# Layer 0's GpSimd order pinned, layer 3's last queries projected beside attention's first stages: a four-layer kernel on one core

## The chip, the core and the metric

The kernel runs on one core of one Trainium2 chip. A core has a matrix engine (TensorE, PE in the profile; its weight loads are PEld), a vector engine (VectorE, DVE), an activation engine (ScalarE, ACT), GpSimd (POOL) and a queue engine (SyncE, SP) that issues DMA transfers. POOL issues transfers too, the indirect ones, which gather rows by an index. Each engine works through its own list of instructions in order, and waits at an instruction until the semaphores that it names have been raised by other engines or by transfers. So an instruction that waits holds everything behind it on its engine.

The metric is the device time of one execution in microseconds (us). Before the change three executions took 2797.17, 2802.5 and 2808.08 us, a median of 2802.5 us. The profiled execution took 2786.42 us. Its span, from the first to the last instruction, is 2784.6 us.

## The reference

x has 32 sequences of 64 tokens with 512 values, 2048 rows. Four layers are each added to x. Two matter here.

```python
# layer 0: cond, then an attention with rope and a mixture of experts
w = weights[subjects]                       # one 64x64 matrix per sequence
out = jnp.einsum('bct,bcd->bdt', x, w)
...
rms = jax.lax.rsqrt(jnp.mean(x * x, axis=-1, keepdims=True) + EPS)
h = x + attention(rmsnorm(x, ln1_w), ...)
out = h + moe(rmsnorm(h, ln2_w), ...)       # 1 shared expert, 2 of 7 routed ones

# layer 3: attention over a paged cache, window 256, then a product in int8
q, k = _rms(q, q_norm_scale), _rms(k, k_norm_scale)
q, k = _rope(q, pos), _rope(k, pos)
k_blocks = k_blocks.at[blk, :, off, :].set(k.transpose(0, 2, 1, 3))
v_blocks = v_blocks.at[blk, :, off, :].set(v.transpose(0, 2, 1, 3))
k_all = k_blocks[block_tables]...
p = jax.nn.softmax(scores, axis=-1)
```

So in layer 0 every pair of sequences needs a weight matrix that is gathered by an index, and in layer 3 every sequence needs the old rows of its cache window, with the new rows put over them.

## The kernel before

The 2048 rows are 16 tiles of 128 rows, two sequences each. The four layers run one after another. A tile framework writes the program: it allocates buffers from pools, adds the waits, and orders the instructions of each engine by its own planning. An instruction given to `pin` (`keep_in_program_order`) isn't moved past others that are so given on its engine; all others may be.

**Layer 0's front** (`layer0`, class `Front`) takes 16 tiles through 13 stages. The list `turns` gives each stage a lag: in step t the stage `mix` works on tile t, `qk_turn` and `scores` on tile t-1, `values`, `out_turn`, `out` and `out_norm` on t-2, `gate_up` and `down` on t-3. So TensorE always has another tile's products to do while one tile's results go through DVE, ACT and POOL.
- `mix` (L422) multiplies the tile by its weights `wbd`. `cond_weights` (L331) makes these on POOL: an indirect DMA brings 128 x 64 values as `wsel` (L284), and two multiplications by a mask (L338) lay them into the two halves of a 128 x 128 block-diagonal tile. `wsel` and `wbd` have two buffers each, and neither is pinned, so the planner put them one or two tiles ahead of their use.
- `rms_scaled` (L311) squares and sums on ACT (L316), forms the mean square `ms` on DVE (L318), raises it to -1/2 on POOL as `rstd` (L308), and scales on DVE (L321). It makes `xn` in `mix` and `hn` in `out`. `norm_turn` then transposes `xn` on TensorE (L414).
- `qkv` adds the two halves of the rope on POOL (L477, `qk`); `qk_turn` transposes the result on TensorE (L414, too).
- `out` adds x and h on POOL (L574).

After the front, experts are computed; layers 1 and 2 follow until 2282 us. In layer 1, `Bridge.work` uses `cond_weights` for its own weights.

**Layer 3** (`layer3`) has two parts. The first projects: `units` is a list of pairs (z, i), where z = 1 is the K/V projection of tile i and z = 0 its query projection; queries follow keys by `LAG` = 5 tiles. In turn u:
- the tile x is transposed (`turn`), and unit u is multiplied (L1803, four matmuls);
- `l3_length` (L1877) makes the norm of its heads: square on ACT, sum on DVE, power on POOL (L1887, `r`);
- unit u-2 is scaled and rotated (`l3_rotate`, L1891): `n` and `tc` on DVE, `ts` on POOL, and unit u-3 gets its sum `qkv` on DVE (L1912);
- a K/V unit's result is written to `newkv` in DRAM by SP (L1829), and for tiles 0 to 7 `old_rows` (L1739) gathers the three old chunks of one sequence's cache;
- a query's result is transposed to heads two turns later (`heads`).

The last five queries (tiles 11 to 15) are only multiplied and copied out as `qlate`; the generator `queries` normalizes, rotates and transposes them later, beside the attention, one of four pieces at every second step.

Then `new_rows` (L1751) gathers rows of `newkv` over the old ones, three gathers a sequence. Most of its indices lie out of bounds and bring nothing. Because it reads `newkv`, it waits for all 16 writes.

The second part is the attention (class `Attend`), in steps s of half a group: `keys` transposes a chunk of the cache (L1936) and makes the mask, `scores` multiplies (L1963) and takes scaled, masked scores and their minimum in one DVE instruction (L1970), then the exponential on ACT (L1974), the division on DVE (L1976, L1977); `turn0` and `turn1` transpose the probabilities (L1985), `values` multiplies by the values (L2010), `product` and its parts (L2032, L2047, L2054) do the output product and the int8 product. Score banks in PSUM are two.

Of the kernel before, what the change touches and what calls it, by code (L numbers as in the profile page):

```python
# [20 lines left out]
P = 128  # L21
# [159 lines left out]
class Prog:  # L181
# [120 lines left out]
            nc.vector.tensor_tensor(out, tp, scale.unsqueeze(2).to_broadcast([P, 4, P]), ALU.mult)  # L302
        return out

    def power(self, pool, src, which, name):

        out = pool.tile(list(src.shape), F32, name=name)
        self.nc.gpsimd.tensor_tensor(out, src, self.c(which)[:, : src.shape[1]], ALU.pow)  # L308
        return out

    def rms_scaled(self, pool, src, name):  # L311

        nc = self.nc
        junk = pool.tile([P, D], F32, name="junk")
        ss = pool.tile([P, 1], F32, name="ss")
        nc.scalar.activation(junk, src, AF.Square, accum_out=ss)  # L316
        ms = pool.tile([P, 1], F32, name="ms")
        nc.vector.tensor_scalar(ms, ss, 1.0 / D, 1e-5, ALU.mult, ALU.add)  # L318
        r = self.power(pool, ms, "nhalf", "rstd")
        out = pool.tile([P, D], F32, name=name)  # L320
        nc.vector.tensor_scalar(out, src, r, None, ALU.mult)  # L321
        return out
# [7 lines left out]

    def cond_weights(self, pool, src, idx, i, out=None):  # L331

        w = pool.tile([P, 64], F32, name="wsel")
        self.gather(w, self.a[src], idx[:, i : i + 1], later=out is not None)
        if out is None:
            out = pool.tile([P, P], F32, name="wbd")
        for k, half in enumerate(("lowhalf", "highhalf")):
            self.nc.gpsimd.tensor_scalar(out[:, 64 * k : 64 * k + 64], w, self.c(half), None, ALU.mult)  # L338
        return out


def layer0(g, w3, pool3):
# [51 lines left out]
class Front:  # L394
# [26 lines left out]

    def mix(self, i):  # L422
        g, nc, sb = self.g, self.g.nc, self.sb
        wbd = g.cond_weights(sb, "wc0", self.at, i)
        if i >= len(self.x):
            self.x.append(g.load_x(sb, g.a["x"], i, 5))
        x = self.x[i]
        o = self.ps.tile([P, D], F32, name="mix", tag="one")
        nc.tensor.matmul(o, wbd, x, start=True, stop=True)
        h = sb.tile([P, D], F32, name="h", bufs=4)  # L430
        nc.scalar.copy(h, o)
        self.keep(i, x=x, h=h, xn=g.rms_scaled(sb, h, "xn"))

    def norm_turn(self, i):
        (xn,) = self.take(i, "xn")
# [4 lines left out]
    def latents(self, i):  # L440
        nc, w = self.g.nc, self.w
        (xnT,) = self.take(i, "xnT")
        lp = self.ps.tile([P, 2, P], F32, name="lp", tag="one")
        for j in range(2):
            for c in range(4):
                nc.tensor.matmul(
                    lp[:, j, :], w["w_lat"][:, c, j * P : (j + 1) * P], xnT[:, c, :], start=c == 0, stop=c == 3
                )
        lat = self.sb.tile([P, 2, P], F32, name="lat")
        nc.scalar.copy(lat, lp)  # L450
        self.keep(i, lat=lat)

    def qkv(self, i):
        g, nc, sb, w = self.g, self.g.nc, self.sb, self.w
        xnT, lat = self.take(i, "xnT", "lat")

        qp = self.ps.tile([P, 2, D], F32, name="qp", tag="big", bufs=2)
        nc.tensor.matmul(qp[:, 0, :], lat[:, 1, :], w["w_q"], start=True, stop=True)
        kv = qp[:, 1, :].rearrange("p (h z d) -> p z h d", h=16, z=2)
        nc.tensor.matmul(  # L460
            kv[:, 0], lat[:, 0, :], w["w_kn"].rearrange("p (h d) -> p h d", h=16), start=True, stop=True
        )
        for c in range(4):
            nc.tensor.matmul(
                kv[:, 1], xnT[:, c, :], w["w_kr"][:, c, :].rearrange("p (h d) -> p h d", h=16),
                start=c == 0, stop=c == 3,
            )
        r = qp.rearrange("p z (h d) -> p (z h) d", h=16)
        qk = sb.tile([P, 32, 32], F32, name="qk")
        nc.scalar.copy(qk[:, :, 0:16], r[:, :, 0:16])  # L470
        cos = g.c("cos").unsqueeze(1).to_broadcast([P, 32, 16])
        sin = g.c("sin").unsqueeze(1).to_broadcast([P, 32, 16])
        nc.vector.tensor_tensor(qk[:, :, 16:32], r[:, :, 16:32], cos, ALU.mult)
        t2 = sb.tile([P, 32, 16], F32, name="t2")
        nc.vector.tensor_tensor(t2[:, :, 0:8], r[:, :, 24:32], sin[:, :, 0:8], ALU.mult)
        nc.vector.tensor_tensor(t2[:, :, 8:16], r[:, :, 16:24], sin[:, :, 8:16], ALU.mult)
        nc.gpsimd.tensor_tensor(qk[:, :, 16:32], qk[:, :, 16:32], t2, ALU.add)  # L477


        vp = self.ps.tile([P, 2, 256], F32, name="vp", tag="one")  # L480
        for b in range(2):
            for odd in range(2):
                nc.tensor.matmul(
                    vp[64 * odd : 64 * odd + 64, b, :], lat[:, 0, 64 * b : 64 * b + 64],
                    w["w_v"][:, 256 * odd : 256 * odd + 256], start=True, stop=True,
                )
        v = sb.tile([P, 2, 256], F32, name="v", bufs=3)
        nc.scalar.copy(v, vp)
        self.keep(i, qk=qk, v=v)
# [501 lines left out]
class Bridge:  # L991
# [11 lines left out]
    def work(self):  # L1003
        g = self.g
        for i in range(NT):
            g.cond_weights(self.pool, "wc1", g.at1, i, self.weights[i])
            yield
        for i in range(NT):
            self.x.append(self.g.load_x(self.pool, self.xs, i, NT, True))
            yield  # L1010
# [698 lines left out]


LAG = 5


def layer3(g, w, xs, xb):
# [3 lines left out]
    with ExitStack() as ctx:  # L1718
# [18 lines left out]
        kvs = []  # L1737

        def old_rows():  # L1739
            b = len(kvs)  # L1740
            if b == B:
                return
            kv = []
            for c in range(3):
                t = cache.tile([CH, D], F32, name="kvt")
                col = c * B + b
                g.gather(t, a["kv"], w["gidx"][0:CH, col : col + 1], later=True)
                kv.append(t)
            kvs.append(kv)

        def new_rows(b):  # L1751
            if b < B:
                for c in range(3):
                    col = c * B + b
                    g.gather(kvs[b][c], new, w["oidx"][0:CH, col : col + 1], bound=N - 1)

        with ExitStack() as c1:
            xp = c1.enter_context(tc.tile_pool(name="l3x", bufs=4, reuse_waits="tile"))
            for part in (slice(0, 4), slice(4, NT)):
# [2 lines left out]
            sb = c1.enter_context(tc.tile_pool(name="l3pj", bufs=2, reuse_waits="tile"))  # L1762
            ps = c1.enter_context(tc.tile_pool(name="l3pq", bufs=3, space=PSUM, reuse_waits="tile"))
            units = [
                (z, i) for t in range(NT + LAG) for z, i in ((1, t), (0, t - LAG)) if 0 <= i < NT
            ]
            xT, held, turned = {}, [], {}

            def turn(i):
                if i < NT:  # L1770
                    xT[i] = g.transpose4(ps, sb, x[i], "xT3", bufs=3, keep=LAG + 3, pin=True)
                    fetch(i + 4)

            def heads(ps, i, q):
                tp = ps.tile([P, 4, P], F32, name="tp", tag="tp", bufs=3)
# [10 lines left out]
            for u in range(len(units) + 5):  # L1786
# [10 lines left out]
                if u < len(units):  # L1797
# [18 lines left out]
                        held.append((pp, out, l3_length(g, sb, pp[:, 0:256])))  # L1816
                    else:
                        held.append((pp, out, l3_length(g, sb, pp)))
                if 0 <= u - 2 < len(units) and held[u - 2]:
                    z, i = units[u - 2]  # L1820
                    pp, out, r = held[u - 2]
                    held[u - 2] = l3_rotate(
                        g, sb, out[:, 0:256] if z else out, pp[:, 0:256] if z else pp, r, tab[z][:, i]
                    )
                if 0 <= u - 3 < len(units) and held[u - 3]:
                    z, i = units[u - 3]
                    out = held[u - 3]()
                    if z:
                        nc.sync.dma_start(out=new[i * P : (i + 1) * P, :], in_=outs[u - 3])  # L1829
                        if i < 8:  # L1830
                            old_rows()
                    else:
                        turned[u - 3] = out
                if u - 5 in turned:
                    heads(ps, units[u - 5][1], turned[u - 5])
            new_rows(0)
# [6 lines left out]
        def queries():  # L1843

            for i, q in slow:
                r = l3_length(g, s1, q)
                yield
                add = l3_rotate(g, s1, q, q, r, tab[0][:, i])
                yield
                add()  # L1850
                yield
                heads(ps, i, q)
                yield

        beside = queries()
        f = Attend(g, w, sb, ps, kvs, qT, xb)

        last = 2 * B - 1
        for s in range(-3, last + 8):
            if s % 2 == 0:  # L1860

                if s >= 4:
                    old_rows()
                new_rows(s // 2 + 4)
            elif s == -3:
                new_rows(2)
            for stage, at in (("keys", s + 3), ("turn0", s), ("scores", s + 2), ("turn1", s)):
                if 0 <= at <= last:
                    getattr(f, stage)(at)
            f.out()  # L1870
            if s >= 2 and s % 2 == 0:
                next(beside, None)
# [1 line left out]
                f.values(s - 1)  # L1874


def l3_length(g, sb, src):  # L1877

    nc = g.nc
    m = src.shape[1] // 64  # L1880
# [3 lines left out]
    nc.vector.tensor_reduce(ss, sq, AX.X, ALU.add)  # L1884
    nc.vector.tensor_scalar(ss, ss, 1.0 / 64, 1e-6, ALU.mult, ALU.add)
    r = sb.tile([P, m], F32, name="r3", bufs=3)
    nc.gpsimd.tensor_tensor(r, ss, g.c("nhalf")[:, 0:m], ALU.pow)  # L1887
    return r


# [204 lines left out]
```

## Time and profile before

The profile is a page about one execution, and a trace that can be asked for stretches of time. "Busy" is the time in which an engine worked, as seen by the profiler.

| what | us |
|---|---|
| median of three executions | 2802.5 |
| the profiled execution | 2786.42 |
| its span | 2784.6 |
| mean granted TensorE clock (1 is full) | 0.959 |

Some stretches, from the windows view, in us from the span's start:

| stretch | length | TensorE busy | DVE busy | ACT busy | POOL busy | granted clock |
|---|---|---|---|---|---|---|
| 0 to 30, layer 0's start | 30 | 7.38 | 2.83 | 2.96 | 8.59 | 1.00 |
| 70 to 280, layer 0's steady tiles | 210 | 199.66 | 128.43 | 85.47 | 49.36 | 1.00 |
| 280 to 370, its last full tiles | 90 | 87.77 | 57.52 | 36.83 | 16.75 | 1.00 |
| 2303 to 2335, layer 3's first units | 32 | 27.38 | 14.24 | 6.04 | 27.80 | 0.97 |
| 2335 to 2398, the later units | 63 | 63.00 | 45.00 | 15.26 | 49.20 | 0.96 |
| 2413 to 2438.4, between the parts | 25.4 | 9.19 | 4.84 | 8.28 | 19.59 | 0.61 |
| 2439 to 2785, the attention | 346 | 286.13 | 211.21 | 166.89 | 157.00 | 0.90 |

A line of a timeline gives the start in us, the busy time in us, the engine, the source line, the operation, what it writes and reads with the shapes, and how many instructions were merged; in brackets the idle time of the engine before it and what ended that idle time. DMA_INDIRECT on POOL is the issuing of a gather, not its transfer. A line of the waits view gives who waited for whom, the total, how many times, and the longest.

### The profile page before, as it was taken

What the parts mean: (1) busy time and instruction counts of PE and PEld (TensorE: products, weight loads), DVE (VectorE), ACT (ScalarE), POOL (GpSimd) and SP (SyncE); (2) the same over time, 40 slices, a digit from 0 to 9 for tenths busy, and PEclk for the clock granted to TensorE, in tenths of its full rate; (3) what the DMA queues carried; (4) which work ended last, traced back from release to release, by engine and by line L of the source; (5) the groups of instructions that cost most, each with busy time, mean ns of one, the idle gap of its engine ahead of it and who ended that gap; (6) DMA issues with size and microseconds to landing.
All of it is one profiled execution on the core that took longest, in us unless ns stands there. A gap on an engine that the chain in (4) does not pass through costs nothing.

```text
span 2784.6 us, 42002 instructions
## 1 busy us (share of the span) xinstructions
PE 2567.1 (92%) x16556; PEld 1640.1 (59%) x16571; DVE 1404.6 (50%) x3479; ACT 748.2 (27%) x1557; POOL 846.8 (30%) x904
## 2 busy tenths in 40 slices
PE   5999998997699999996899999999999999788878
PEld 4777765654555655654666666667666654344444
DVE  3666655734754333334455544445554416466656
ACT  2444430112211121111222222222222212354444
POOL 2222114624222223213122222222222108656550
PEclk9999999998699999998999999999999999889898
DMA  2233224446545965534010000001000025124340
GB/s 93 91 124 127 96 77 164 156 148 191 169 166 195 345 228 211 201 125 156 17 38 27 28 27 28 27 31 50 27 27 27 31 78 182 53 74 115 89 112 29
DMA packets 107078, 291.21 MB, mean 105 GB/s; under 512 B 20682, under 2 KB 21482, under 8 KB 99569
## 3 DMA queue, kind: packets, MB, share of 16 engines
q1 hardware_dynamic: 71232, 193.46, 19.5%
q0 software_dynamic: 35056, 89.13, 11.0%
q10 hardware_dynamic: 576, 5.77, 0.5%
q8 instruction: 135, 2.21, 0.3%
q14 instruction: 79, 0.64, 0.1%
HBM read 216.76 MB, written 87.56 MB: 109 GB/s over the span
## 4 chain that ended last, share of the span: by engine, by line
PE 48%; DVE 3%; issue 2%; POOL 1%; DMA 1%; another core or an unknown queue 1%; ACT 0%; SPq 0%; ACTq 0%; POOLq 0%; DVEq 0%
PE lp L1356 8%; PE out L1499 8%; PE zp L1433 8%; PE hp L1465 3%; PE gp L1488 2%; PE pp L1803 2%; PE y L2032 2%; PE op L2010 2%; PE sp L1963 2%; PE yp L1301 2%; PE pT L1985 2%; PE ep L1442 1%; PE kp L1936 1%; PE ap L1289 1%; PE csum L1452 1%
## 5 line engine op out<-in xcount | busy, mean ns | idle before, releaser
L910 PE MATMUL gu<-xT,wt 128*128 128x320 f32 x1472 | 407.1, 434 | 0.0
L910 PEld LDWEIGHTS gu<-xT,wt 128*128 128x128 f32 x1472 | 277.7, 191 | 119.5 <-issue 11.4
L1356 PEld LDWEIGHTS lp<-xnT,sb_mu 128*128 128x128 f32 x2048 | 235.7, 193 | 8.8 <-issue 6.7
L1356 PE MATMUL lp<-xnT,sb_mu 128*128 128x128 f32 x2048 | 238.6, 277 | 1.5 <-DVE xnT L256 0.8
L929 PE MATMUL y<-wt,hT 128*128 128x512 f32 (+1 forms) x552 | 238.7, 606 | 0.1
L1499 PE MATMUL out<-sb_w,gT 128*128 128x512 f32 x512 | 233.6, 599 | 0.0
L1433 PE MATMUL zp<-sb_w,xnT 128*128 128x512 f32 x512 | 226.5, 592 | 0.0
L1492 DVE COPY gT<-gp 128x512 f32<-128x512 f32 x64 | 44.3, 692 | 235.4 <-PE gp L1488 235.0
L284 POOL DMA_INDIRECT xr<-rows,stok x115 | 110.2, 958 | 154.7 <-PE tp L891 86.1
L1433 PEld LDWEIGHTS zp<-sb_w,xnT 128*128 128x128 f32 x512 | 93.7, 190 | 104.7 <-issue 100.9
L1499 PEld LDWEIGHTS out<-sb_w,gT 128*128 128x128 f32 x512 | 93.4, 190 | 103.5 <-issue 95.2
L929 PEld LDWEIGHTS y<-wt,hT 128*128 128x128 f32 (+1 forms) x552 | 80.0, 171 | 104.9 <-issue 88.4
L659 POOL TENSOR_TENSOR ga<-ga,sg 128x320 f32<-128x320 f32 x64 | 55.2, 863 | 283.4 <-ACT sg L655 281.3
L284 POOL DMA_INDIRECT yk<-ys,slot x96 | 99.5, 1036 | 123.9 <-SPq L798 65.2
L1510 POOL TENSOR_TENSOR xt<-xt,bc_bias 128x512 f32<-128x512 f32 x16 | 20.3, 1270 | 360.1 <-DMA x<-xt 360.1
L1470 ACT ACTIVATE h<-hp 128x512 f32<-128x512 f32 x128 | 69.5, 594 | 214.2 <-PE hp L1465 214.0
L1970 DVE CUSTOM_DVE_ANT_0 s<-sp,mask 128x336 f32<-128x336 f32 x128 | 61.4, 504 | 124.2 <-PE sp L1963 42.8
L284 POOL DMA_INDIRECT kvt<-kv,gidx x96 | 94.9, 989 | 93.6 <-PE op L2010 64.7
L1394 POOL TENSOR_TENSOR eT<-eT,inv 128x512 f32<-128x512 f32 x64 | 71.6, 1120 | 151.2 <-DVE inv L1393 149.3
L284 POOL DMA_INDIRECT kvt<-newkv,oidx x96 | 98.3, 1024 | 38.9 <-issue 29.9
L2032 PE MATMUL y<-sb_w_o,oT 128*128 128x512 f32 x128 | 74.4, 667 | 22.5 <-DVE y3s L1516 16.0
L891 PEld LDWEIGHTS tp<-sb_cst,xr 128*128 128x128 f32 x460 | 53.7, 147 | 65.4 <-issue 32.3
(379 smaller groups left out, 4616.2 us busy)
## 6 DMA issues: line engine op xcount, KB each, us to landing
wt<-w_e SPq DMA_DIRECT2D x32, 1538.0 KB
ys<-yo SPq DMA_DIRECT2D x115, 256.0 KB
ys<-zero SPq DMA_DIRECT2D x10, 2048.0 KB
xt<-x SPq DMA_DIRECT2D x62, 256.0 KB
wt<-w_e SPq DMA_DIRECT2D x7, 1536.0 KB
x<-xt SPq DMA_DIRECT2D x32, 256.0 KB
sb_w<-w SPq DMA_DIRECT2D x5, 1024.0 KB
rows<-hn SPq DMA_DIRECT2D x16, 256.0 KB
```

What stands on the lines that cost most here:

```text
L284: ins = self.nc.gpsimd.indirect_dma_start(out=out, out_offset=None, in_=src, in_offset=bass.IndirectOffsetOnAxis(ap=idx, axis=0), **kw)
L910: nc.tensor.matmul(o, wj[:, c, ic * P : (ic + 1) * P], xT[:, c, :], start=c == 0, stop=c == 3)
L929: nc.tensor.matmul(y[row : row + n, :], hTs[u][:, ic, col : col + n], wd[:, ic, :], start=ic == 0, stop=ic == 1,)
L1301: g.first(c, nc.tensor.matmul(yp, self.xT[:, c, :], w["w_2"][:, c, :], start=c == 0, stop=False))
L1356: g.first(e + c, nc.tensor.matmul(lp[:, e, :], w["mu"][:, c, (4 * q + e) * P : (4 * q + e + 1) * P], self.xnT[:, c, :], start=c == 0, stop ...
L1394: g.pin(nc.gpsimd.tensor_tensor(e3, e3, inv.unsqueeze(2).to_broadcast([P, 8, T]), ALU.mult))
L1433: g.first(c, nc.tensor.matmul(zp, self.xnT[:, c, :], w["w1"][:, c, cols], start=c == 0, stop=c == 3))
L1465: g.first(e + b, nc.tensor.matmul(hp[:, b, e, :], self.ews[q][r, e, :], self.z[q][r, e * P : (e + 1) * P], start=True, stop=True))
L1470: g.pin(nc.scalar.activation(self.hs[q][b], hp[:, b], AF.Gelu))
L1499: g.first(e, nc.tensor.matmul(self.out, self.gTs[q][:, e, :], w["w2"][:, 4 * q + e, :], start=q + e == 0, stop=q + e == 6 and q == 3))
L1970: nc.vector.tensor_tensor_reduce(p, sps[j], self.masks[2 * i + half], -0.0625, 3.0e38, ALU.add, ALU.min, m)
L2032: nc.tensor.matmul(yp, self.oT[i][:, c // 2, c % 2, :], w["w_o3"][:, c, :], start=c == 0, stop=c == 3)
```

## The change

In layer 0, `mix` no longer makes its own tile's weights. After it has given out the norm of tile i, it asks for the gather of tile i+1's weights (`weights`), and after `latents` of tile i the two multiplications lay them (`lay`). The gather, the multiplications, `rstd` of `xn` and the rope's sum `qk` on POOL are pinned. Tile 0's weights are made at once.

In layer 3:
- `old_rows` gathers one chunk instead of three, and is called once in every turn from 3 to 26, 24 times as before in sum; in the attention it is called three times where it was called once;
- `new_rows` is pinned;
- the queries of the last three tiles (`LAST`) are no longer units. Their x is transposed into parts of K's rope table that are no longer needed, and `project` multiplies them at the attention's steps -3, -2 and -1, with the banks of `y3` and `acc`;
- the last K/V unit is rotated one turn after its product instead of two, and in every turn the sums of older units are given out before the rotation of newer ones;
- `queries` takes five turns for a query instead of four, and its power on POOL is pinned.

```diff
     def mix(self, i):
         g, nc, sb = self.g, self.g.nc, self.sb
-        wbd = g.cond_weights(sb, "wc0", self.at, i)
+        if i == 0:
+            self.weights(0)
+            self.lay()
+        wbd = self.wbd
...
-        self.keep(i, x=x, h=h, xn=g.rms_scaled(sb, h, "xn"))
+        self.keep(i, x=x, h=h, xn=g.rms_scaled(sb, h, "xn", True))
+        self.weights(i + 1)
+
+    def weights(self, i):
+
+        self.asked = self.g.cond_weights(self.sb, "wc0", self.at, i) if i < NT else None
+
+    def lay(self):
+        if self.asked:
+            self.wbd = self.asked(self.sb.tile([P, P], F32, name="wbd"))
...
         self.keep(i, lat=lat)
+        self.lay()
...
-        nc.gpsimd.tensor_tensor(qk[:, :, 16:32], qk[:, :, 16:32], t2, ALU.add)
+        g.pin(nc.gpsimd.tensor_tensor(qk[:, :, 16:32], qk[:, :, 16:32], t2, ALU.add))
```

`cond_weights` and the power:

```diff
     def cond_weights(self, pool, src, idx, i, out=None):
 
         w = pool.tile([P, 64], F32, name="wsel")
-        self.gather(w, self.a[src], idx[:, i : i + 1], later=out is not None)
-        if out is None:
-            out = pool.tile([P, P], F32, name="wbd")
-        for k, half in enumerate(("lowhalf", "highhalf")):
-            self.nc.gpsimd.tensor_scalar(out[:, 64 * k : 64 * k + 64], w, self.c(half), None, ALU.mult)
-        return out
+        self.gather(w, self.a[src], idx[:, i : i + 1], later=True)
+
+        def lay(out):
+            for k, half in enumerate(("lowhalf", "highhalf")):
+                self.pin(self.nc.gpsimd.tensor_scalar(out[:, 64 * k : 64 * k + 64], w, self.c(half), None, ALU.mult))
+            return out
+
+        return lay
```

Layer 3:

```diff
         def old_rows():
-            b = len(kvs)
-            if b == B:
-                return
-            kv = []
-            for c in range(3):
-                t = cache.tile([CH, D], F32, name="kvt")
-                col = c * B + b
-                g.gather(t, a["kv"], w["gidx"][0:CH, col : col + 1], later=True)
-                kv.append(t)
-            kvs.append(kv)
+            if not kvs or len(kvs[-1]) == 3:
+                if len(kvs) == B:
+                    return
+                kvs.append([])
+            t = cache.tile([CH, D], F32, name="kvt")
+            col = len(kvs[-1]) * B + len(kvs) - 1
+            g.gather(t, a["kv"], w["gidx"][0:CH, col : col + 1], later=True)
+            kvs[-1].append(t)
...
-                    g.gather(kvs[b][c], new, w["oidx"][0:CH, col : col + 1], bound=N - 1)
+                    g.gather(kvs[b][c], new, w["oidx"][0:CH, col : col + 1], bound=N - 1, later=True)
...
-                (z, i) for t in range(NT + LAG) for z, i in ((1, t), (0, t - LAG)) if 0 <= i < NT
+                (z, i) for t in range(NT + LAG) for z, i in ((1, t), (0, t - LAG)) if 0 <= i < NT - (not z) * LAST
             ]
+            lag = [1 if unit == (1, NT - 1) else 2 for unit in units]
...
+                    j = 4 * (i - NT + LAST)
+                    xT[i] = tab[1][:, j : j + 4, :]
+                    g.evac(xT[i], tp)
...
+                for k, (z, i) in enumerate(units[: u + 1]):
+                    if not held[k]:
+                        continue
+                    if u == k + lag[k]:
+                        pp, out, r = held[k]
+                        held[k] = l3_rotate(
+                            g, sb, out[:, 0:256] if z else out, pp[:, 0:256] if z else pp, r, tab[z][:, i]
+                        )
+                    elif u == k + lag[k] + 1:
+                        out = held[k]()
+                        if z:
+                            nc.sync.dma_start(out=new[i * P : (i + 1) * P, :], in_=outs[k])
+                        else:
+                            turned[k] = out
+                if 3 <= u < 27:
+                    old_rows()
...
+        def project(i):
+
+            pp = ps.tile([P, D], F32, name="pp3", tag="y3" if i % 2 else "acc", bufs=1)
+            for c in range(4):
+                g.first(c, nc.tensor.matmul(pp, xT[i][:, c, :], wq[:, c, :], start=c == 0, stop=c == 3))
+            out = wp.tile([P, D], F32, name=f"qlate{i}")
+            nc.scalar.copy(out, pp)
+            slow.append((i, out))
...
+            if s == -3:
+                project(NT - LAST)
...
+            if -3 < s < LAST - 3:
+                project(NT - LAST + s + 3)
```

## The prediction

> **What bounds the kernel now.** I read the page's busy row first, then its slices, then the waits of TensorE, then the timelines of the two places where TensorE waits.
>
> ```profile
> PE 2567.1 (92%) x16556; PEld 1640.1 (59%) x16571; DVE 1404.6 (50%) x3479; ACT 748.2 (27%) x1557; POOL 846.8 (30%) x904
> PE   5999998997699999996899999999999999788878
> ```
>
> TensorE is the bound: 217 us of the span are left to it, and the second line, its busy tenths in 40 slices of 70 us, puts part of them at the very start and in the last seven slices. No matmul is removed, so only its waits can be won. The change touches layer 0's front (0 to 414 us) and layer 3 (2282 us to the end). TensorE's waits in the first 560 us, as (total, times, longest):
>
> ```profile
> PE tp L414 <- DVE xn L321: 22.9, 15, 8.5
> PE mix L429 <- DMA sb_w_v<-w_v: 12.8, 1, 12.8
> PE tp L414 <- POOL qk L477: 3.7, 1, 3.7
> ```
>
> The transpose of xn waits at nearly every tile. Why, POOL's timeline shows (start, us), at the first tiles and at a later one:
>
> ```profile
> 20.10 0.87 POOL L338 TENSOR_SCALAR wbd<-wsel,sb_cst 128x64 f32<-128x64 f32 x2 [3.02 <-DMA wsel<-wc,i_cond]
> 21.24 1.01 POOL L284 DMA_INDIRECT wsel<-wc,i_cond  x1 [0.27 <-POOL wbd L338]
> 22.28 0.60 POOL L308 TENSOR_TENSOR rstd<-ms,sb_cst 128x1 f32<-128x1 f32 x1
> 35.06 0.87 POOL L338 TENSOR_SCALAR wbd<-wsel,sb_cst 128x64 f32<-128x64 f32 x2 [12.18 <-PE mix L429]
> 36.21 1.04 POOL L284 DMA_INDIRECT wsel<-wc,i_cond  x1 [0.28 <-POOL wbd L338]
> 37.28 1.29 POOL L477 TENSOR_TENSOR qk<-qk,t 128x512 f32<-128x512 f32 x1
> 240.65 1.04 POOL L284 DMA_INDIRECT wsel<-wc,i_cond  x1 [0.28 <-POOL wbd L338]
> 241.71 0.60 POOL L308 TENSOR_TENSOR rstd<-ms,sb_cst 128x1 f32<-128x1 f32 x1
> ```
>
> rstd and qk, which TensorE waits for, stand behind weights of later tiles. In layer 3, TensorE, then POOL, then DVE:
>
> ```profile
> 2334.55 1.09 PE L1777 MATMUL tp<-sb_cst,qkv 128*128 128x128 f32 x4 [4.62 <-DVE qkv L1912]
> 2438.43 1.50 PE L1985 MATMUL pT<-sb_cst,s 128*112 128x128 f32 x6 [5.97 <-DVE s L1977]
> 2406.90 1.09 POOL L284 DMA_INDIRECT kvt<-newkv,oidx  x1 [0.39 <-issue]
> 2436.80 0.99 POOL L284 DMA_INDIRECT kvt<-newkv,oidx  x1 [0.30 <-issue]
> 2424.07 0.51 DVE L1970 CUSTOM_DVE_ANT_0 s<-sp,mask 128x336 f32<-128x336 f32 x1 [3.46 <-remote]
> 2430.40 0.51 DVE L1970 CUSTOM_DVE_ANT_0 s<-sp,mask 128x336 f32<-128x336 f32 x1 [5.81 <-remote]
> ```
>
> There is one stall of 4.62 us in the projections. Then, from 2413.0 to 2438.4, TensorE works 9.2 of 25.4 us. In it POOL issues 24 gathers of new rows without a break (2406.90 to 2437.8, one each 1.30 us), and DVE gets only six L1970 started (2418.43, 2419.84, 2424.07, 2430.40, 2433.90, 2437.46), though their scores lay ready; with the last gather it runs on. So what ends this gap is the end of the burst, and the burst's start is the landing of the last newkv write.
>
> **Layer 0, part by part.** The built order of the changed kernel on POOL is, for a tile: rstd of xn, gather of the next wsel, its two wbd halves, memset, x+h, rstd of hn, qk. No instruction is added.
> - First tile: ms is ready at 16.48 (DVE 16.33 + 0.15), rstd began at 22.28. It now follows wbd 0 at once: 5.8 us.
> - First qk: its operand t is ready at 34.89 (DVE 34.48 + 0.41), it began at 37.28, behind a wbd and a gather: 2.35 us of the 3.67 us wait. What is late next is mix 1, right ahead of it.
> - Tile 2: ms 54.89, rstd 55.99: 1.05 us of its 1.84.
> - The steady tiles: nine waits of 1.14 to 1.16 us (75.23 to 267.27). The last four tiles have no later weights to gather, so their rstd follows ms directly, and they wait 0.55 to 0.57. That is the changed order, already in this trace: 9 x 0.58 = 5.2 us. The rest, ACT's and DVE's chain from mix to xn, stays.
> - Against it: at tile 1 one scores matmul now precedes the xn transposes and waits for both copies (0.59 and 0.68 us, half seen): -0.8.
>
> Sum 13.6 us. The added wait is wbd's for its own wsel gather, just issued. Behind it on POOL stand memset, x+h and rstd of hn. The gather ends at 242.7 and x+h begins at 255.7: 13 us of cover. [...]
>
> **Layer 3's projections.** Old rows were three gathers in a run beside a K/V unit (for a pair of units POOL needs 3 x 1.25 + 1.04 + 0.72 + 1.63 + 1.26 = 8.4 us; TensorE 7.74). Now it is one a unit: 7.15 us a pair, and POOL keeps up. The 4.62 us wait goes: 4.6 us (bounds 2 to 4.6). [...] The row says: tc of 256 columns takes 0.42 us alone and 0.42 beside a gather (2306.20), but 1.14 beside POOL's own multiplication (2398.67). [...] I take 0. The last three transposed x go into rows of K's table that were read units ago: no wait.
>
> **The last K/V unit.** Its add ended on DVE near 2403.98, behind another unit's n, ss and tc (0.68, 0.67, 1.45 us); rotated a unit earlier it precedes them: 3.0 us (bounds 0 to 5). The write's landing (2.00) is unchanged, and SP's order is the same: from 2363 to 2404 it holds only such writes, so nothing stands before it. The pinned r of a late query now stands within the burst: -1.65 us, since the burst ends later by it. So the burst ends 4.6 + 3.0 - 1.65 = 6.0 us sooner.
>
> **The three late projections** (each 3.44 us of TensorE, 10.3 together) leave the front and go beside the burst. That by itself wins nothing: TensorE would only reach the wait sooner. It costs nothing either, for 16 us are idle there; without that cover the 10.3 us would merely return. But the first scores then come when gather 6 has landed, near 2410 (start 2399.3, five pitches of 1.30, 1.0 of issue, 3.0 of landing by the chain's row), not 2418, and DVE's trickle has 2 us more; its new order also does s0 and s1's divisions (1.8 us, done after the burst before). I take 2.5 us (bounds -2, as ACT's copies of qlate stand before its exponentials, to 7).
>
> For the clock, the row of granted clock from 2420 to 2460 us has 0.68, that is some 26 us at half. [...] The trace prices it less: from 2438.4 slow forms (kp 0.77 us for three) end at 2445.91 (0.51), 6 us of busy TensorE at half, so 3 us. [...]
>
> Layer 3: 6.0 + 2.5 = 8.5 us. The beside-work of the attention has five turns a query, done by step 50 instead of 40; the earliest need of the last is step 58. Its r of 1.65 us lie in POOL's idle 189 of 346 us: nothing.
>
> **Sum.** 13.6 + 8.5 = 22 us. Against the profiled execution (2786.4 us, span 2784.6) that gives 2764. The median of the runs is 2802.5, 16 us above that execution; taken from it, **2780**.
>
> **Rivals.**
> 1. *The burst decides alone* (0.18): the last write or the trickle doesn't come earlier, or the copies take back what they win. For: DVE starts one L1970 in 3.5 us whatever waits. Against: the write's place in the order is plain. Layer 0 alone, with 1 us: 2788.
> 2. *The gap closes further* (0.15): projections keep the clock up and softmax is well under way at the burst's end; layer 3 gives 16: 2772.
> 3. *POOL is blocked in layer 0* (0.05): wbd waits for a late wsel under the 2 MB zero writes, with hn's rstd behind it. It decides from a landing 14.6 us after issue (13 of cover, and 22 us of gain over 14 tiles); at 16 us: 2802.5 - 22 + 14 x 3 = 2822. Against: the longest such wait in the trace is 5.9 us.
> 4. *The order takes no effect* (0.03): 2800. Against: the built order shows it.
>
> The forecast has 0.59; its own range is 2770 to 2790. About 0.5% (14 us) is what runs of this kernel, 2797 to 2808, can tell from no change. From the cases: faster 0.82, same 0.13, slower 0.05. The range, 2762 to 2796, adds to the forecast's the second rival and most of the first.
>
> **What would show it.** Right: waits for xn near 0.57 at all steady tiles, about 11 us in sum; the first rstd near 16.5; no wait of 4 us in the projections; the first newkv gather some 8 us sooner against the layer's start, and the first op L2010, 162 us after the layer's start now, near 154. Wrong: wbd waits that reach x+h; a first gather unmoved; L1970 started more rarely, or attention (346 us from 2439) longer by more than 3.

## The result

| | median of 8 runs | lowest to highest | profiled execution: span, mean granted clock |
|---|---|---|---|
| before | 2802.0 us | 2797.2 to 2808.1 | 2784.6 us, 0.959 |
| changed | 2777.7 us | 2770.1 to 2791.0 | 2783.5 us, 0.956 |

The ratio is 0.9909, with a 95% interval of 0.9887 to 0.9931: 24.3 us faster. The two profiled executions do not show that: they differ by 1.1 us, since before's (2786.4) lies 15.6 us below its median and the changed one's (2785.3) 7.6 us above. So the gain has to be read by stages.

### The profile after

First the busy row of TensorE and its busy tenths in 40 slices, from the page of the changed kernel.

```profile
PE 2575.4 (93%) x16556; PEld 1641.2 (59%) x16571; DVE 1401.2 (50%) x3479; ACT 749.3 (27%) x1557; POOL 846.4 (30%) x904
PE   7999979996799999979899999999999999787778
```

The first slice rose from 5 to 7. The last six slices still hold 7s and 8s: the end of the kernel is no fuller than it was.

Next TensorE's waits in layer 0's front (total, times, longest).

```profile
PE tp L419 <- DVE xn L323: 8.9, 12, 2.8
PE tp L419 <- ACT kT L423: 1.5, 3, 0.5
PE tp L419 <- POOL qk L495: 1.4, 1, 1.4
```

GpSimd's timeline (start, us) at the first tile and at a steady one:

```profile
16.39 0.58 POOL L308 TENSOR_TENSOR rstd<-ms,sb_cst 128x1 f32<-128x1 f32 x1 [3.77 <-DVE ms L320]
17.17 1.29 POOL L284 DMA_INDIRECT wsel<-wc,i_cond  x1 [0.19 <-issue]
...
85.52 0.55 POOL L308 TENSOR_TENSOR rstd<-ms,sb_cst 128x1 f32<-128x1 f32 x1 [1.65 <-DVE ms L320]
86.24 1.27 POOL L284 DMA_INDIRECT wsel<-wc,i_cond  x1 [0.17 <-issue]
89.01 0.87 POOL L341 TENSOR_SCALAR wbd<-wsel,sb_cst 128x64 f32<-128x64 f32 x2 [1.50 <-DMA wsel<-wc,i_cond]
```

rstd now comes first and waits for ms alone; the gather follows, and wbd waits 1.50 us for it while nothing is late on GpSimd. The waits ahead of the transposes of xn are down from 22.9 us to 10.4: the 12 of the first row and the three of 0.49 us in the second, which stand at the same transposes and which the view puts to ACT's kT.

In layer 3, the end of the projections and the first new rows on TensorE and GpSimd, then the scores that DVE takes up, and the first product with V:

```profile
2382.00 0.63 PE L1805 MATMUL tp<-sb_cst,qkv 128*128 128x128 f32 x4 [2.30 <-DVE qkv L1958]
2382.82 1.04 POOL L284 DMA_INDIRECT kvt<-newkv,oidx  x1 [2.39 <-DMA newkv<-qkv]
2404.94 0.51 DVE L2016 CUSTOM_DVE_ANT_0 s<-sp,mask 128x336 f32<-128x336 f32 x1 [8.03 <-remote]
2408.50 0.51 DVE L2016 CUSTOM_DVE_ANT_0 s<-sp,mask 128x336 f32<-128x336 f32 x1 [3.04 <-PE sp L2009]
2417.08 0.51 DVE L2016 CUSTOM_DVE_ANT_0 s<-sp,mask 128x336 f32<-128x336 f32 x1 [5.75 <-remote]
2420.63 1.54 PE L2056 MATMUL op<-pTs,kvt 112*64 112x128 f32 x12
```

The stall of 4.62 us in the projections is gone; a smaller one of 2.30 us stands at their end. DVE still starts its L2016 (L1970 before) rarely while the new rows are gathered: twice from 2393 to 2417 us. Layer 3 begins at 2266.9 us, 15.4 us sooner than before, and its first op comes 153.7 us after that instead of 162.3. Those are 24.0 us. From there to the end the profiled execution takes 362.9 us, before's 340.0, and that is where the profiles lose the gain again. Whether this is a cost of the change or scatter was the first question.

### The profile page after: what moved, and what is told of

It is laid out like the page before. It is cut to its first block, busy times and chain, and to the rows that moved or that the text cites. A ratio compares the mean times of both kernels' runs of the same rounds, so it can differ in the third digit from the quotient of the medians.

```text
span 2783.5 us, 42018 instructions
## 1 busy us (share of the span) xinstructions
PE 2575.4 (93%) x16556; PEld 1641.2 (59%) x16571; DVE 1401.2 (50%) x3479; ACT 749.3 (27%) x1557; POOL 846.4 (30%) x904
## 4 chain that ended last, share of the span: by engine, by line
PE 49%; DVE 2%; issue 2%; another core or an unknown queue 1%; DMA 1%; ACT 1%; POOL 0%; SPq 0%; ACTq 0%; POOLq 0%; DVEq 0%
PE lp L1374 8%; PE out L1517 8%; PE zp L1451 8%; PE pp L1831 3%; PE hp L1483 3%; PE gp L1506 2%; PE y L2078 2%; PE sp L2009 2%; PE yp L1319 2%; PE op L2056 2%; PE pT L2031 2%; PE ep L1460 1%; PE kp L1982 1%; PE ap L1307 1%
## 5 line engine op out<-in xcount | busy, mean ns | idle before, releaser
L2016 DVE CUSTOM_DVE_ANT_0 s<-sp,mask 128x336 f32<-128x336 f32 x128 | 61.2, 503 | 138.5 <-PE sp L2009 40.0
L1412 POOL TENSOR_TENSOR eT<-eT,inv 128x512 f32<-128x512 f32 x64 | 71.6, 1119 | 152.2 <-DVE inv L1411 151.2
L2020 ACT ACTIVATE s<-s,m 128x336 f32<-128x336 f32 x128 | 72.9, 572 | 74.5 <-DVE m L2016 53.3
```

The source lines that it names most:

```text
L1412: g.pin(nc.gpsimd.tensor_tensor(e3, e3, inv.unsqueeze(2).to_broadcast([P, 8, T]), ALU.mult))
L2020: nc.scalar.activation(p, p, AF.Exp, bias=m, scale=-1.0, accum_out=tot)
```

## The experiments

They were made in three sets, and the kernel before ran beside each: it took 2703.6 us in the first set, 2699.8 in the second and 2803.2 in the third, where the result above had 2802.0. The first two sets ran on one chip and the third on another; for the result no chip is on record. So every kernel's time is compared with before of its own set only, and the absolute times expected in the first set, which start from the result's 2802 us, were missed by about 100 us. The table has the landmarks of each profile, in us after the start of layer 3 (its first transpose of x).

| kernel | set | layer 3 starts | first new-row gather | 24th | first op | first op to the end | ratio to before, 95% |
|---|---|---|---|---|---|---|---|
| before | result | 2282.2 | 124.7 | 154.6 | 162.3 | 340.0 | |
| changed | result | 2266.9 | 115.9 | 147.4 | 153.7 | 362.9 | 0.9909 (0.9887 to 0.9931) |
| l0_only | 1 | 2260.2 | 124.3 | 154.4 | 148.2 | 273.3 | 0.9933 (0.9919 to 0.9948) |
| l3_only | 1 | 2281.7 | 116.3 | 148.0 | 145.0 | 273.3 | 0.9978 (0.9968 to 0.9988) |
| unbound | 1 | 2259.0 | 116.3 | 165.0 | 142.9 | 269.0 | 0.9899 (0.9884 to 0.9915) |
| spread | 1 | 2265.7 | 116.2 | 165.6 | 139.6 | 272.0 | 0.9893 (0.9876 to 0.9909) |
| before_again | 2 | 2278.4 | 124.7 | 154.6 | 147.4 | 276.1 | |
| after_again | 2 | 2260.7 | 116.0 | 147.7 | 145.0 | 272.4 | 0.9927 (0.9905 to 0.9949) |
| rows_lag | 2 | 2258.0 | 117.0 | 148.5 | 148.9 | 268.3 | 0.9924 (0.9905 to 0.9943) |
| ss6 | 2 | 2263.0 | 115.9 | 148.3 | 139.1 | 262.8 | 0.9868 (0.9844 to 0.9893) |
| ss6_rows | 3 | 2269.6 | 117.3 | 148.8 | 152.2 | 349.7 | 0.9902 (0.9880 to 0.9925) |
| no_lag | 3 | 2270.4 | 115.6 | 147.4 | 150.7 | 353.2 | 0.9930 (0.9903 to 0.9956) |
| spread6 | 3 | 2282.1 | 115.9 | 163.5 | 139.8 | 322.6 | 0.9760 (0.9732 to 0.9788) |
| uncovered | 3 | 2391.8 | 116.2 | 147.8 | 151.9 | 360.9 | 1.0343 (1.0316 to 1.0371) |

### Each part alone, and both kernels again

l0_only has the diff's edits outside layer 3 alone, l3_only those inside it.

> Layer 0's part alone; layer 3 as before. Theory 1 (the gain is 16.7 us of layer 0's front plus 8.6 us of layer 3 up to its first product with V, and the attention after that is no longer on average; the 22.9 us by which it was longer in the one profile are scatter between executions): 2802 - 17 = 2785 us, layer 3 starts 17 us sooner than before, and the attention's length from first op to the end lies anywhere between 340 and 363 us. Theory 2 (the changed layer 3 really makes the attention 22.9 us longer): then this kernel, without that part, is 14 us faster than the whole change, 2764 us.

> Layer 3's part alone; layer 0 as before. Theory 1: 2802 - 8.6 = 2793 us; first op 154 us after the layer's start. Theory 2: 2802 - 8.6 + 22.9 = 2816 us, slower than before, with an attention of 363 us.

> The kernel before, profiled a second time. If the attention of 340 us in its first profile belongs to the kernel, it is found again; if to the place and time of that execution, it is found like that of the two partial kernels (273 us), with the start of layer 3 unmoved at 2282 us.

> The whole change, profiled a second time beside the others. Theory 1: it is the sum of its two parts: layer 3 starts 16 us sooner than before, the first op comes about 3 us sooner after the layer's start where the hand-offs are prompt (8.6 us where they are late), and the attention is as long as before's of the same runs: 20 to 25 us faster.

Layer 0's part won 17.8 us (expected 17) and layer 3's 7.4 us (8.6). Theory 2, by which layer 3's part makes the kernel slower, falls for this set: the ratio of l3_only is below 1 by its whole interval. The sum of the parts, 25.3 us, is near what the result has, 24.3. In the second set the changed kernel won 18.2 us, less than the 20 to 25 expected; its interval, 0.9905 to 0.9949, takes in the result's ratio.

before_again settles what the 340 us were. Its layer 3 begins at 2278.4 us and its first gather comes at +124.7, as in the first profile; then all of it is quicker: first op at +147.4, and 276.1 us from there. The difference of 82.8 us between the two profiles of one and the same kernel lies in layer 3 after its projections, but for the 3.8 us by which the layer begins sooner. after_again has 272.4 us from the first op on, 3.7 less than before_again, so in this set the change does not make the attention longer. For the result's own setting the medians say it: before's profiled execution was 15.6 us below its median and the changed one's 7.6 above, 23.2 together. So the 22.9 us by which the changed kernel's attention was longer there are scatter of two single executions, as far as medians can tell, and not a cost of the change.

### A wait that the change added

In the profile of l3_only a chain showed up that the prediction had not: GpSimd's r (the power in a late query's norm), pinned behind 18 gathers, then DVE's ss (the sum of squares of another late query), then TensorE's scores.

```profile
2421.23 1.67 POOL L1913 TENSOR_TENSOR r<-ss,sb_cst 128x8 f32<-128x8 f32 x1
2422.93 0.69 DVE L1910 TENSOR_REDUCE ss<-sq 128x8 f32<-128x512 f32 x1 [6.22 <-POOL r L1913]
2424.29 1.64 PE L1991 MATMUL sp<-kT,qT 64*128 64x336 f32 x4 [4.08 <-DVE m L1998]
```

ss has three buffers. The fourth late query's ss needs the first one's back, which r still has to read; DVE's order is fixed, so everything behind that ss waits as well. In before_again DVE waits so for r once, 2.0 us. ss6 takes the wait away by giving ss six buffers, and rows_lag leaves the wait and takes the moved projections away.

```diff
-    ss = sb.tile([P, m], F32, name="ss3", bufs=3)
+    ss = sb.tile([P, m], F32, name="ss3", bufs=6)
```

```diff
-LAST = 3
+LAST = 0
...
-            if s == -3:
+            if LAST and s == -3:
                 project(NT - LAST)
```

> The changed kernel with six buffers instead of three for ss of the lengths: the fourth late query's ss on DVE no longer waits for the r that the change pinned behind 18 gathers on GpSimd. If that wait costs what the profile of layer 3's part alone shows (DVE idle 6.2 us, TensorE 4.1 us on m): the first op comes 3 to 5 us sooner than in the whole change and the time falls by as much. If something else (the landing of the rows, PSUM) is just behind it: no difference.

> The changed kernel with no projection moved into the attention (the last three queries are projected in the front, as before); old rows one at a unit, the last K/V unit rotated a unit sooner, and layer 0's part kept. If the moved projections win nothing by themselves (the prediction's step): equal to the whole change within 3 us, the first newkv gather as early against the layer's start up to the 10 us of projections that now stand before it. If they are what counts (they fill TensorE while the first rows are fetched): 8 to 12 us slower than the whole change.

DVE's waits for r, and TensorE's for what DVE then owes, from 100 us after layer 3's start to the end, first in after_again, then in rows_lag:

```profile
DVE ss L1928 <- POOL r L1931: 10.9, 2, 5.5
PE pT L2031 <- DVE pTs L2036: 3.9, 1, 3.9
PE sp L2009 <- DVE m L2016: 3.2, 1, 3.2
```

```profile
DVE ss L1928 <- POOL r L1931: 17.0, 2, 10.7
PE sp L2009 <- DVE m L2016: 10.5, 2, 10.2
PE pT L2031 <- DVE pTs L2036: 4.7, 1, 4.7
```

In ss6 all three lines are gone; the longest of what is left on TensorE are these:

```profile
PE kp L1982 <- DMA kvt<-newkv,oidx: 3.7, 3, 3.2
PE qtp L2093 <- DVE yq L1535: 2.4, 1, 2.4
PE tp L1805 <- DVE qkv L1958: 2.3, 1, 2.3
```

ss6 took 2665.8 us where the changed kernel took 2681.6: 15.8 us less, three times the most that was expected, and the intervals of the two ratios do not touch. In the profiles the first op came 5.9 us sooner, just over the expectation, and from there to the end ss6 took 9.6 us less. The second such wait stood there (3.9 us of TensorE in after_again): for the same 1834 matmuls TensorE is idle 3.3 us less in ss6 and busy 252.4 us instead of 258.7, at a granted clock of 0.99 instead of 0.96.

rows_lag was as fast as the whole change (2680.0 and 2681.6), though its TensorE waits 10.2 us for m where the other waits 3.2. So most of the 10.3 us of moved projections (7.0) seem to stand in that wait. Whether they win anything once the wait is gone was to be shown by ss6_rows (both edits above).

> Six ss buffers as in ss6, but the last three queries projected in the front, as before. The prediction's step (moved projections win nothing by themselves; they only fill a wait): with the wait of ss gone there is nothing to fill but the landing of the first rows (2 to 4 us), so this kernel is 0 to 4 us slower than ss6. If the 10.3 us of projections are hidden by the move: 8 to 10 us slower.

It fell in the third set, where ss6 was not run, so the comparison it was made for is missing. Beside the changed kernel's own ratio, 0.9909 in the result, its 0.9902 (0.9880 to 0.9925) shows no gain: in this setting six buffers together with projections in the front are worth nothing that can be seen, so the 15.8 us are shown for the second set alone. Whether the moved projections win anything stays open.

### The last K/V unit's rotation

```diff
-            lag = [1 if unit == (1, NT - 1) else 2 for unit in units]
+            lag = [2 for unit in units]
```

> The changed kernel with the last K/V unit rotated two units after its product, like all others. The prediction's step: the last write lands 3.0 us later, so that the first newkv gather starts at 119 us after the layer's start instead of 116; the first op then comes 3 us later (148 instead of 145) and the time rises by 3. Rival: TensorE has late projections to do meanwhile, and the first op does not move.

The first gather came at +115.6, not at 119: the earlier rotation does not bring it forward. The time, 0.9930 of before's, cannot be told from the changed kernel's 0.9909 in the result; the changed kernel itself was not run in this set. SP's writes of new K/V show what did move. The last one leaves at +122.1 in before, at +113.1 in no_lag and at +111.9 in the changed kernel. So nine of the ten microseconds are there without the earlier rotation. Part of them is the stall that is gone (4.6). Another part is DVE's order, first in before, then in no_lag (n is the next query's, the qkv of 128x128 the last K/V unit's add; in before it is the first two of the four merged):

```profile
2400.93 0.68 DVE L1897 TENSOR_TENSOR n<-pp,r 128x512 f32<-128x512 f32 x1
...
2403.50 1.15 DVE L1912 TENSOR_TENSOR qkv<-tc,ts 128x128 f32<-128x128 f32 x4
```

```profile
2382.66 0.49 DVE L1958 TENSOR_TENSOR qkv<-tc,ts 128x128 f32<-128x128 f32 x2 [0.62 <-POOL ts L1949]
2383.07 0.68 DVE L1943 TENSOR_TENSOR n<-pp,r 128x512 f32<-128x512 f32 x1
```

The query's n, ss and tc (2.8 us) stood before the add and now stand behind it. Both n and the add are pinned, so it is the order in which a turn gives them out that counts: before, the rotation of the newer unit and then the sum of the older one; after the change, the sum first. no_lag keeps that edit, and so does rows_lag, which has the projections in front and starts its gathers at +117.0. No run takes it away alone.

The earlier rotation sends the write 1.2 us sooner still, but the gather comes 4.0 us after it in the changed kernel and 2.6 in no_lag. In after_again, where the landing is on record, the last write landed 3.0 us after it left and the first of the last four 2.1. Why it lands later there, no run here shows.

### The run of gathers

spread makes the gathers of each later group wait for a copy of their indices that DVE does at that group's step. In its profiles 12 gathers still run in a row, not the nine expected; the others follow in groups.

```diff
+                if hold is not None:
+                    now = hold.tile([P, 3], I32, name="now", bufs=4)
+                    g.pin(nc.vector.tensor_copy(now, w["oidx"].rearrange("p (c b) -> p c b", c=3)[:, :, b]))
+                    at = [now[0:CH, c : c + 1] for c in range(3)]
...
-                new_rows(s // 2 + 4)
+                new_rows(s // 2 + 4, sb)
```

> The changed kernel, with each later group of three new-row gathers made to wait for a 3-column copy of its indices that DVE does at that group's own step, so that only nine gathers are free to go at once and the other 15 of the first 24 follow at their steps. If the burst as such ends the gap: the first op comes 146 us after the layer's start instead of 154 (15 gathers of 1.3 us less in front, and some of them still within the gap). If these gathers hold the hand-offs up wherever they stand, the 8 us come back in the attention: 2772 to 2785 us in all; if only the long burst does: 2765 us. If the gap is bound by the landing of the first rows and not by the burst: first op unmoved at 154.

> Six ss buffers and the spread new-row gathers together. If what the spreading won was only that the pinned r no longer stood behind 18 gathers: no better than ss6, within 3 us. If the run of 24 gathers holds TensorE's readers up by itself: 4 to 8 us faster than ss6.

> The changed kernel, but the gathers of new rows carry no bound: their indices are clamped to the last row, so that every row of a block that is not new takes new row 2047 (the values are other ones, the number of instructions the same, and each gather moves all its 112 rows). Theory A (the hand-offs from TensorE to the other engines come late because of the bound that these gathers carry on GpSimd): DVE and ACT run on during the 24 gathers of the gap, TensorE's wait before the first op falls from some 25 us to under 8, and the stalls of 3 to 4 us beside each later group of three or four go: 24 groups, 40 to 80 us in all, 2700 to 2740 us. Theory B (it is any gather from the new rows, or their data, not the bound): the gap and the stalls stay, 2770 to 2795 us.

unbound's edit:

```diff
-    nc.vector.scalar_tensor_tensor(w["oidx"], win, -1.0, none, ALU.add, ALU.add)
+    nc.vector.scalar_tensor_tensor(none, win, -1.0, none, ALU.add, ALU.add)
+    nc.vector.tensor_single_scalar(w["oidx"], none, float(N - 1), ALU.min)
...
-                    g.gather(kvs[b][c], new, w["oidx"][0:CH, col : col + 1], bound=N - 1, later=True)
+                    g.gather(kvs[b][c], new, w["oidx"][0:CH, col : col + 1], later=True)
```

unbound leaves out the choice of rows: rows that are not wanted go over the old ones too, and only its time is of use. It ran in the first set, where nothing came late: in l0_only and l3_only the first op comes 6.2 and 3.0 us ahead of the 24th gather, not behind it, so that the run of gathers does not end the gap. There it could not tell its theories apart, and what it took, 2677.5 us, is what the two parts won together (2703.6 less 25.3 is 2678.3). It is inconclusive; whether the bound plays a part stays open.

spread in the same set has the first op at +139.6 where l3_only has it at +145.0, and that is what ss6 reaches (+139.1) by its buffers alone: r is no longer behind 18 gathers. That part needs no burst to explain it, and spread's time, 2675.3 us, is not clear of the 2678.3 either.

spread6 (spread and six buffers) ran in the third set, where DVE comes late as in the result. ss6_rows, of the same set, has the six buffers too, but neither the spacing nor the moved projections. The stretch from just before the first gather over 39.5 us, in ss6_rows and in spread6 (window and length, then busy us of TensorE, its weight loads, DVE, ACT and GpSimd; granted clock; DMA share; GB/s):

```profile
2385.10:2424.60 39.50, 24.84 (x86) 12.80 (x84) 12.14 (x45) 16.08 (x40) 25.57 (x25) 0.67 0.18 50
```

```profile
2397.60:2437.10 39.50, 36.60 (x193) 19.16 (x191) 22.69 (x86) 26.14 (x68) 25.20 (x25) 0.91 0.23 62
```

With GpSimd equally busy (25.2 and 25.6 us) TensorE works 36.6 instead of 24.8 us and DVE 22.7 instead of 12.1. In ss6_rows and no_lag the first op comes at +152.2 and +150.7, in spread6 at +139.8, with the 24th gather only at 163.5. The time fell to 2735.9 us, 67 us below before of its set and 39 below ss6_rows. So neither six buffers with the projections in front (ss6_rows) nor moved projections with three buffers (no_lag) free this gap. This speaks for the prediction's reading, by which in this setting an unbroken run of gathers holds up what reads TensorE's results, and spacing them frees it. It is not the whole proof: ss6, which has six buffers and moved projections without the spacing, and spread were not run in this set.

### The cover of the weights' gather

uncovered asks for a tile's weights and lays them out at the tile's own mix.

```diff
-        if i == 0:
-            self.weights(0)
-            self.lay()
+        self.weights(i)
+        self.lay()
...
-        self.weights(i + 1)
...
         self.keep(i, lat=lat)
-        self.lay()
```

> The changed kernel, but each tile's weights are gathered and laid out at the tile's own mix, not a tile ahead; rstd and qk stay pinned. On GpSimd's built order gather and wbd of a tile now stand right behind the qk of the tile before, which begins only about when mix is to begin (106.17 and 106.36 in the profile of the changed kernel). From that profile: qk's end 107.45, the gather 1.27, its landing 1.50 later, wbd 0.87: mix at 111.1 instead of 106.4, 4.8 us a tile, 15 tiles, 72 us slower than the whole change. [...] If another engine is the bound of layer 0, so that GpSimd's delay is absorbed: under 15 us.

It was 99 us slower than before of its set, and its layer 3 begins 121 us later than no_lag's, where 72 were expected. TensorE's waits in its layer 0 (the probs of the first line is a memset of 0.09 us right behind wbd on GpSimd; what mix reads is wbd):

```profile
PE mix L436 <- POOL probs L607: 53.6, 12, 5.9
PE mix L436 <- POOL wbd L341: 24.9, 4, 12.4
```

One steady tile on its timeline:

```profile
198.48 1.05 POOL L284 DMA_INDIRECT wsel<-wc,i_cond  x1 [0.16 <-issue]
...
202.34 0.87 POOL L341 TENSOR_SCALAR wbd<-wsel,sb_cst 128x64 f32<-128x64 f32 x2 [2.81 <-DMA wsel<-wc,i_cond]
...
203.26 2.07 PE L436 MATMUL mix<-xt,wbd 128*128 128x512 f32 x2 [3.83 <-POOL probs L607]
```

And the row of the stretch from the first mix to the end of the last router product, with the same 4002 matmuls (columns as above), in it and then in the changed kernel:

```profile
12.44:523.06 510.62, 420.60 (x4002) 313.64 (x4002) 239.86 (x606) 151.90 (x269) 88.90 (x124) 0.87 0.22 77
```

```profile
12.67:406.62 393.95, 374.16 (x4002) 281.59 (x4002) 238.81 (x606) 152.16 (x269) 92.74 (x124) 1.00 0.29 100
```

The front takes 116.7 us more. The mix waits are 78.5 us, 66 without the first tile's 12.4, near the 72 expected. Most of the rest is the clock: TensorE is busy 420.6 us instead of 374.2 for the same matmuls, 46 more, at a clock of 0.87 instead of 1.00 (mix takes 2.07 us, 1.10 in the changed kernel). Twelve of the 15 waits last 3.6 to 6.0 us, three only 2.6 to 2.8; beside one of the three, of 2.56 us, which ends at 423.45, the clock is 0.50 from 422.2 to 432.2 us. All 15 together cost about 0.7 of their length again, 46 us for 66.

## Why the prediction was right

The time was forecast at 2780 us and came to 2777.7; the gain at 22 us, and it was 24.3. For layer 0 the mechanism was right. That the sum came so near is in part luck: layer 0 gave more than its 13.6 us, and in layer 3 one term was laid to the wrong edit and one wait was not seen. By its steps:

- **Layer 0, 13.6 us forecast.** The last router product came at 406.34 instead of 423.04 us: 16.7. The waits moved as worked out: the first for xn from 8.53 to 2.81 us (5.7 of 5.8), qk's from 3.67 to 1.35 (2.3 of 2.35), tile 2's by 0.98 (1.05), and the new wait for tile 1's scores is 0.68 (0.8). The steady tiles fell to 0.49 us, but for one of 0.86, a little below the 0.57 that served as model. The term left out was the clock: it was granted at 0.95 in the first 70 us before and at 1.00 now, and tile 0's qk transposes and scores with tile 1's lp take 5.0 us instead of 7.4. Over all profiles the last router product comes at 423 to 426 us in three with the old front and at 406 to 413 in ten with the new one, some 14.5 us apart in the middle, so 16.7 is at the upper end of what the front won.
- **The cover of wbd.** Its waits are 30.5 us on GpSimd, 15 of them, the longest 4.7, and nothing behind them was late: right. In before's profile a gather issued at 16.13 us had its wbd begin at 20.10, 4.0 us later. Without the cover, and with the gather behind qk on GpSimd (uncovered), the front took 117 us more, through mix's waits and the clock.
- **The projections' stall, 4.6 us.** Gone, but 2.3 us stand at their end.
- **The last K/V unit, 3.0 us.** A term laid to the wrong edit: the write did go sooner, by more than that, but without the earlier rotation too (no_lag); the add passes the query's n, ss and tc because the older sums are given out first. And the landing, taken as unchanged, grew from about 2 to 3 us where it is on record. The first gather came 8.8 us sooner where "some 8" was forecast.
- **r within the burst, -1.65 us.** It took 1.67 us there. What was missed is who stands behind r: DVE's ss, for want of a buffer, twice. The prediction asked that question of POOL's waits, and not of the pinned r.
- **The spread gathers beside DVE, 0.** From 20 to 120 us after the layer's start DVE is busy 64.5 us in l0_only and 63.4 in l3_only: nothing added in sum.
- **The moved projections, 0.** rows_lag bears it out for the changed kernel: with or without them the same time. They fill a wait, partly one that the change itself made.
- **The first op, 154 us after the layer's start.** 153.7. The 8.5 us of layer 3 were 8.6 in the profile, 7.4 by the part alone. The clock's 3 us are no term of that sum; over 39.5 us from just before the first gather the granted clock was 0.65 before and 0.72 now. But in the second set the first op came only 2.4 us sooner (147.4 to 145.0): there the end of the burst does not bound it.
- **"Attention longer by more than 3 us" as a sign against it.** It was longer by 22.9 us in the profile, and the sign was a bad one: it compares single executions, and the two profiled ones lay 15.6 us below and 7.6 above their medians. Two profiles of the kernel before, in different settings, differ by 64 us there.

Of the rivals, the burst did not take the copies' gain back; wbd was never late; the order took effect. That the end of the burst ends the gap fits the result's setting and the third set (spread6), and not the other two sets, where the first op comes ahead of the 24th gather (by 7 us in before_again).

## What to carry to other kernels

Pinning an instruction in an in-order queue fixes the place of everything that needs its result, and of everything that needs a buffer back from it: before pinning, count the buffers between the producer and the pinned reader, since three more of a tile of 32 bytes a partition were worth 15.8 us in one setting here. Weigh a wait on TensorE at more than its length when it comes back at every tile, since the 15 waits of 2.6 to 6 us in uncovered together cost about 0.7 of their length again through the clock. And compare stages of two profiles only when a second profile of the same kernel says how far the stage scatters.

## What was not expected of the hardware

The same kernel, with the same instructions, took 2802 us in two settings and 2700 in two others. Of the 82.8 us between before's two profiles 79 lie after the start of layer 3's gathers of new rows. Before's first profile has ten waits of TensorE of 2 us and more after the first op, 26.9 us in all; before_again has one, 2.4 us, at the end. Of the 26.9 us some 13 lie beside gathers of new rows, which are under way in about 94 of the 340 us (72 of 1.30), and 2.0 beside the as many gathers of old rows. That is not a clean division: in the changed kernel's profile of the result it is 12.6 and 7.0 of 35.2 us. In the second set the gathers have the same pace (1.30 us apart in after_again), and the changed kernel has two such waits, 6.3 us. The slow settings and the quick ones ran on different chips, as far as is on record; whether the chip is the cause, and what on it, no run here shows.
